# A selective-scan and attention kernel: the state input product on GpSimd, exp(delta A) in PSUM, y summed by plain matmuls

## The chip, the core and the metric

The kernel runs on one core of a Trainium2 chip, in fp32 throughout. The metric is device time in microseconds (us) of one launch. The engines are named as the profile names them: PE is TensorE (PEld its weight loads), DVE is VectorE, ACT is ScalarE, POOL is GpSimd, and SP is SyncE, whose queue issues most of the DMA.

## The reference, cut to what matters

```python
# per image of 8, over the 1024 pixels as a sequence; run forward and, flipped, backward
u, z     = split(rmsnorm(x) @ in_proj)                 # 384 channels each
u        = silu(causal_conv1d(u, 4 taps) + bias)
dt, B, C = split(u @ x_proj)                           # 24, 16 and 16 columns
delta    = softplus(dt @ dt_proj + b)
for each of 16 states n, along the sequence t:
    h[n] = exp(delta * A[n]) * h[n] + (delta * u) * B[n]
    y   += h[n] * C[n]
y        = (y + u * D) * silu(z);  global = y @ out_proj
local    = sigmoid(depthwise_conv3x3(x_norm) + b) * x_norm
x        = x + res_scale * (scale_mod * (fwd + bwd) + local)
# then, on tokens: layernorm, causal attention with RoPE, residual; layernorm, FFN 384-1536-384, residual
```

There are 8 images of 384 channels by 32 x 32 pixels. The change lies in the conv1d, in the loop over states, and in what leads from y to the output projection.

## The kernel before, in words

Channels lie on the partitions: 384 channels are NC = 3 blocks (`cc`) of P = 128. The 1024 positions of an image are two halves of HB = 512. `STEPS` names the four scan steps of an image: forward over half 0 and half 1, then backward over half 1 and half 0. The numbers 0 to 3 (`si`) are these steps. Each step goes through NS = 16 states, so that the whole kernel has 32 steps and 512 states.

One state in `scan` is this. ACT writes `da` = exp(delta * A[n]), three 128x512 activations (L346) into an SBUF tile with two buffers. DVE multiplies `du` = delta * u by B[n] over all three blocks at once (L348, 128x1536). Here B[n] is spread over the partitions by PE transposes into the PSUM bank `bb` (L335). DVE then runs three 512-long scans in place (L356). In steps 0 and 2 a small copy keeps the last column for the next step (L359). DVE multiplies by C[n] from PSUM bank `cb` (L360). Last, PE adds the product into the PSUM tile `y` by twelve 128x128 transposes that accumulate (L365), so that `y` comes out with positions on the partitions.

`prepare` makes the inputs of the next step. It computes the conv1d on PE as four matmuls with diagonal matrices for each block (L266), then silu on ACT (L270), the projection to dt, B and C, and delta through Abs, Relu, Exp and Ln (L295 to L302) and an add on DVE (L305). `gate` computes silu(z) (L247, L251). `project` transposes the gated y back (L378, L381) and applies the output projection (L386, L388). `local` is the 3x3 convolution on DVE (L228). The attention and the FFN of the image before are the generator `tail`.

The scan calls `pump` after each state. It advances the generators beside it: one step each of `prepare` and, in steps 1 and 2, of `local`, and three of `tail`. The framework orders each engine's instructions ahead of time from priorities (order in the program) and from when buffers come free[...]. Tiles with one tag share that tag's buffers. The PSUM pools take eight 512-column tiles (banks): three for `y`, one each for `bb` and `cb`, and three for everything else (`bank()`, tag `w`).

The y tile of one step is followed at its end by these lines, which also take the PE between steps:

```python
if si >= 2:
    szf = sz.rearrange("p i c -> p (i c)")
    nc.vector.scalar_tensor_tensor(szf, yv, gs, szf, ALU.mult, ALU.mult)
    ...
    project(b, h, sz, t1)
```

Of the kernel before, what the change touches and what calls it, by code (L numbers as in the profile page):

```python
# [24 lines left out]

P = 128
HB = 512
STEPS = [(0, 0), (0, 1), (1, 1), (1, 0)]


@with_exitstack
def conv_attn_kernel(
# [36 lines left out]
    l1 = ctx.enter_context(tc.tile_pool(name="l1", bufs=1))  # L69
    ps_y = ctx.enter_context(tc.tile_pool(name="ps_y", bufs=1, space=bass.MemoryType.PSUM))  # L70
    ps_b = ctx.enter_context(tc.tile_pool(name="ps_b", bufs=1, space=bass.MemoryType.PSUM))
    ps_w = ctx.enter_context(tc.tile_pool(name="ps_w", bufs=3, space=bass.MemoryType.PSUM))

    count = [0]

    def name(s):
        count[0] += 1
        return f"{s}_{count[0]}"
# [52 lines left out]

    nc.scalar.activation(nega, nega, AF.Exp)
    nc.vector.tensor_scalar_mul(nega, nega, -1.0)


    cdiag = const.tile([P, NC, 4, P], F32, name="cdiag")
    for cc in range(NC):
        for k in range(4):
            nc.gpsimd.tensor_scalar(cdiag[:, cc, k], ident, cw[:, cc, k : k + 1], None, ALU.mult)


    ddiag = const.tile([P, NC, P], F32, name="ddiag")
# [96 lines left out]

    def gate(b, h):  # L240

        sz = l0.tile([P, NT, C], F32, tag="sz", name=name("sz"))
        for i in range(NT):
            pz = bank()
            at = h * HB + i * P
            for cc in range(NC):
                nc.tensor.matmul(  # L247
                    pz[:, :C], xn_t[b][:, cc, at : at + P], win[:, cc, C:],
                    start=cc == 0, stop=cc == NC - 1,
                )  # L250
            nc.scalar.activation(sz[:, i], pz[:, :C], AF.Silu)  # L251
        return sz


    def prepare(b, step, res):

        d, h = step
        t0 = h * HB
        u = u_t[b]
        uc = l0.tile([P, NC, HB], F32, tag="uc", name=name("uc"))  # L260
        for cc in range(NC):
            pc = bank()
            for k in (3, 2, 1, 0):
                s = k - 3 if d == 0 else 3 - k
                a, e = max(t0, -s), min(t0 + HB, L - s)
                nc.tensor.matmul(  # L266
                    pc[:, a - t0 : e - t0], cdiag[:, cc, k], u[:, cc, a + s : e + s],
                    start=k == 3, stop=k == 0,
                )
            nc.scalar.activation(uc[:, cc], pc, AF.Silu, bias=v_cb[:, cc : cc + 1])  # L270
            yield
        px = bank()
        for cc in range(NC):
            nc.tensor.matmul(px[:NX], xp[:, cc], uc[:, cc], start=cc == 0, stop=cc == NC - 1)
        xd = l0.tile([NX, HB], F32, tag="xd", name=name("xd"))
        nc.scalar.copy(xd, px[:NX])
        yield

        pt = bank()
        for i in range(NT):  # L280
            nc.tensor.transpose(
                pt[:, i * NX : (i + 1) * NX], xd[:, i * P : (i + 1) * P], ident[:NX, :NX]
            )
        bc = l0.tile([P, NT, 2 * NS], F32, tag="bc", name=name("bc"), bufs=2)
        nc.scalar.copy(bc, pt[:, : NT * NX].rearrange("p (i e) -> p i e", i=NT)[:, :, R:])
        yield

        dl = l0.tile([P, NC, HB], F32, tag="dl", name=name("dl"), bufs=2)
        sps = []
        for cc in range(NC):  # L290
            pd = bank()
            nc.tensor.matmul(pd, dtw[:, cc * P : (cc + 1) * P], xd[:R], start=True, stop=True)
            sp = l0.tile([P, HB], F32, tag="tmp", name=name("sp"), bufs=4)
            bias = v_dtb[:, cc : cc + 1]
            nc.scalar.activation(sp, pd, AF.Abs, bias=bias)  # L295
            nc.scalar.activation(dl[:, cc], pd, AF.Relu, bias=bias)  # L296
            sps.append(sp)
            yield
        for sp in sps:
            nc.scalar.activation(sp, sp, AF.Exp, scale=-1.0)  # L300
        for sp in sps:
            nc.scalar.activation(sp, sp, AF.Ln, bias=ones[:, 0:1])  # L302
        yield
        for cc, sp in enumerate(sps):
            nc.vector.tensor_add(dl[:, cc], dl[:, cc], sp)  # L305
        res.append((uc, bc, dl))

    carry = const.tile([P, NS, NC], F32, name="carry")

    def block(y, i, cc):  # L310

        return y[:, i * C + cc * P : i * C + (cc + 1) * P]

    def opens(i, cc):

        return (i * C + cc * P) % HB == 0

    def scan(step, prep, y, first, last, save, restore, pump):

        d, h = step  # L320
        uc, bc, dl = prep
        du = l0.tile([P, NC, HB], F32, tag="du", name=name("du"))
        nc.vector.tensor_mul(du, dl, uc)
        for i in range(NT):
            for cc in range(NC):
                nc.tensor.matmul(  # L326
                    block(y, i, cc), uc[:, cc, i * P : (i + 1) * P], ddiag[:, cc],
                    start=first and opens(i, cc), stop=False, skip_group_check=True,
                )

        def spread(what, at):

            pb = ps_b.tile([P, HB], F32, tag=what, name=name(what))
            for i in range(NT):
                nc.tensor.transpose(  # L335
                    pb[:, i * P : (i + 1) * P],
                    bc[:, i, at : at + 1].to_broadcast([P, P]),
                    ident,
                )
            return pb.unsqueeze(1).to_broadcast([P, NC, HB])  # L340

        bb, cb = spread("bb", 0), spread("cb", NS)
        for n in range(NS):
            da = l0.tile([P, NC, HB], F32, tag="da", name=name("da"), bufs=2)
            for cc in range(NC):
                nc.scalar.activation(da[:, cc], dl[:, cc], AF.Exp, scale=nega[:, cc, n : n + 1])  # L346
            hs = l0.tile([P, NC, HB], F32, tag="hs", name=name("hs"), bufs=3)
            nc.vector.tensor_mul(hs, du, bb)  # L348
            if n + 1 < NS:
                bb = spread("bb", n + 1)  # L350
            for cc in range(NC):
                o, a = hs[:, cc], da[:, cc]
                if d:
                    o, a = o[:, ::-1], a[:, ::-1]
                init = carry[:, n, cc : cc + 1] if restore else 0.0
                nc.vector.tensor_tensor_scan(o, a, o, init, ALU.mult, ALU.add)  # L356
            if save:
                at = 0 if d else HB - 1
                nc.vector.tensor_copy(carry[:, n], hs[:, :, at])  # L359
            nc.vector.tensor_mul(hs, hs, cb)  # L360
            if n + 1 < NS:
                cb = spread("cb", NS + n + 1)
            for cc in range(NC):
                for i in range(NT):
                    nc.tensor.matmul(  # L365
                        block(y, i, cc), hs[:, cc, i * P : (i + 1) * P], ident,
                        start=False, stop=last and n == NS - 1,
                        is_transpose=True, skip_group_check=True,
                    )
            pump()  # L370

    def project(b, h, yzT, t1):

        yz = l0.tile([P, NC, HB], F32, tag="hs", name=name("yz"), bufs=3)
        for cc in range(NC):
            pt = bank()
            for i in range(NT):
                nc.tensor.transpose(  # L378
                    pt[:, i * P : (i + 1) * P], yzT[:, i, cc * P : (cc + 1) * P], ident
                )  # L380
            nc.scalar.copy(yz[:, cc], pt)  # L381
        for i in range(NT):
            cols = slice(i * P, (i + 1) * P)
            po = bank()
# [204 lines left out]
    for b in range(NB):  # L589
# [4 lines left out]
        for si, step in enumerate(STEPS):  # L594
            d, h = step
            prep = preps.pop()
            if si == 1:
                run(rest)
                yv = y1 = ps_y.tile([P, NC * HB], F32, tag="y", name=name("y"))
            elif si == 2:  # L600
                yv = y1
            else:
                yv = ps_y.tile([P, NC * HB], F32, tag="y", name=name("y"))
            if si >= 2:
                sz = gate(b, h)
            if si == 3:
                for k in range(0, NC * HB, HB):
                    nc.tensor.matmul(
                        yv[:, k : k + HB], ident, y0[:, k : k + HB],
                        start=True, stop=False, skip_group_check=True,  # L610
                    )
            nxt = (b, STEPS[si + 1]) if si < 3 else (b + 1, STEPS[0])
            side = []
            if si == 0:
# [15 lines left out]
                if g is not local_b or si == 2:  # L630
                    run(g)
            if si == 0:
                y0 = l0.tile([P, NC * HB], F32, tag="y0", name=name("y0"))
                nc.scalar.copy(y0, yv)
            if si >= 2:
                szf = sz.rearrange("p i c -> p (i c)")
                nc.vector.scalar_tensor_tensor(szf, yv, gs, szf, ALU.mult, ALU.mult)
                if t1 is None:
                    run(tail)
                    t1 = l1.tile([P, L // P, C], F32, tag="t1", name=name("t1"))  # L640
# [78 lines left out]
```

## Time and profile before

| | |
|---|---|
| median of 3 runs | 5035.7 us (5034.59 to 5038.16) |
| the profiled execution's own time | 5038.16 us |
| its span, first to last instruction | 5036.1 us |
| DVE, PE, ACT, POOL busy in the span | 4349.1, 3936.4, 2812.2, 46.3 us |
| mean granted TensorE clock | 0.849 |
| one image in the steady state (L356 of step 0 to the next image's) | 1802.2 to 2408.7 us: 606.5 us |

"Busy" is time in which the engine ran an instruction. A group of the profile is all instructions of one source line, engine and shape, with total busy time, the mean of one in ns, and the idle time of the engine just before them with the work that ended it. On DVE, instructions run back to back overlap by some 0.1 us, so that the sum of durations is a little over the time they take. A plain fp32 matmul leaves two records in the trace, a transpose one.

### The profile page before, as it was taken

The page shows a single profiled execution, that of the slowest core. Times are in us where ns is not written, and L with a number is a line of the kernel's source. Part 1 is how long each engine was busy: PE and PEld are TensorE (multiplying, and loading weights), DVE is VectorE, ACT ScalarE, POOL GpSimd, SP SyncE. Part 2 cuts the span into 40 slices and gives each one's busy share as a digit, 9 for nine tenths or more (in the row PEclk, how much of TensorE's full clock was granted, in tenths as well). Part 3 has the DMA queues.
Part 4 walks back from the last instruction along what each step waited for, and adds up shares of the span by engine and source line. Part 5 has one row for each costly group of instructions (what it writes and reads, how often), then busy time and mean ns, then how long its engine had stood idle before and what let it go on. Part 6 is the DMA issues. An engine that isn't in the chain of part 4 may idle for free.

```text
span 5036.1 us, 44726 instructions
## 1 busy us (share of the span) xinstructions
PE 3936.4 (78%) x17360; PEld 2525.6 (50%) x17360; DVE 4349.1 (86%) x4404; ACT 2812.2 (56%) x3988; POOL 46.3 (1%) x87
## 2 busy tenths in 40 slices
PE   6757788777887778867888778887788777887777
PEld 3545554455545555455554555545554455545542
DVE  6998999889998899898898899988999889998841
ACT  4543567635685446844567446673567635685222
POOL 0000000000000000000000000000000000000000
PEclk8867898888997889878998789986898878997678
DMA  1000000000000000000000000000000000000000
GB/s 42 1 0 7 7 1 7 7 7 7 1 7 7 7 7 1 13 1 7 7 1 13 7 1 7 1 13 7 7 1 7 7 7 7 1 7 7 0 1 13
DMA packets 19289, 31.69 MB, mean 6 GB/s; under 512 B 5356, under 2 KB 6276, under 8 KB 19076
## 3 DMA queue, kind: packets, MB, share of 16 engines
q1 hardware_dynamic: 17152, 28.64, 1.6%
q8 instruction: 136, 2.23, 0.2%
q14 instruction: 77, 0.63, 0.0%
q10 hardware_dynamic: 1924, 0.19, 0.0%
HBM read 16.24 MB, written 12.58 MB: 6 GB/s over the span
## 4 chain that ended last, share of the span: by engine, by line
DVE 59%; PE 20%; ACT 12%; issue 8%; DMA 0%; ACTq 0%; DVEq 0%; POOL 0%; POOLq 0%
DVE hs L356 28%; DVE hs L360 12%; DVE hs L348 11%; ACT da L346 3%; PE w L386 3%; PE w L247 2%; DVE sg L228 2%; ACT L346 2%; PE y L365 2%; PE w L544 2%; PE y L326 1%; ACT gl L543 1%; ACT L543 1%; PE w L505 1%; PE w L555 1%
## 5 line engine op out<-in xcount | busy, mean ns | idle before, releaser
L346 ACT ACTIVATE da<-dl,nega 128x512 f32<-128x512 f32 x1536 | 1020.4, 714 | 1241.0 <-DVE hs L356 1143.6
L365 PE MATMUL y<-ident,hs 128*128 128x128 f32 x6144 | 1018.6, 328 | 110.3 <-DVE hs L360 110.3
L348 DVE TENSOR_TENSOR hs<-du,bb 128x1536 f32<-128x1536 f32 x512 | 891.5, 1741 | 212.9 <-PE bb L335 212.1
L365 PEld LDWEIGHTS y<-ident,hs 128*128 128x128 f32 x6144 | 921.2, 174 | 162.9 <-DVE hs L360 123.5
L356 DVE TENSOR_TENSOR_SCAN hs<-da,carry,hs 128x512 f32<-128x512 f32 x768 | 937.2, 1269 | 26.8 <-ACT da L346 21.1
L360 DVE TENSOR_TENSOR hs<-hs,cb 128x1536 f32<-128x1536 f32 x512 | 894.3, 1747 | 49.9 <-PE cb L335 39.8
L356 DVE TENSOR_TENSOR_SCAN hs<-da,hs 128x512 f32<-128x512 f32 x768 | 894.6, 1209 | 6.8
L335 PE MATMUL cb<-ident,bc 128*128 128x128 f32 x2048 | 404.8, 329 | 465.0 <-DVE hs L360 460.1
L335 PEld LDWEIGHTS cb<-ident,bc 128*128 128x128 f32 x2048 | 266.6, 161 | 666.3 <-DVE hs L360 628.3
L335 PE MATMUL bb<-ident,bc 128*128 128x128 f32 x2048 | 373.3, 309 | 217.9 <-DVE hs L348 203.4
L335 PEld LDWEIGHTS bb<-ident,bc 128*128 128x128 f32 x2048 | 263.1, 154 | 372.5 <-DVE hs L348 309.7
L346 ACT ACT_TABLE_LOAD x287 | 368.2, 1283 | 135.8 <-DVE hs L356 131.4
L266 PE MATMUL w<-u,cdiag 128*128 128x512 f32 (+3 forms) x768 | 360.2, 603 | 3.0 <-ACT dl L296 3.0
L228 DVE SCALAR_TENSOR_TENSOR sg<-xn,dww,sg 128x496 f32<-128x496 f32 (+3 forms) x384 | 275.2, 720 | 1.5
L544 PE MATMUL w<-gl,cp1s 128*32 128x512 f32 x384 | 217.3, 685 | 47.6 <-ACT gl L543 47.6
L505 PE MATMUL w<-v,pT 128*128 128x384 f32 x576 | 231.9, 554 | 28.2 <-ACT pT L501 26.4
L266 PEld LDWEIGHTS w<-u,cdiag 128*128 128x128 f32 x768 | 140.7, 195 | 142.3 <-issue 132.0
L203 PE MATMUL w<-xn,win 128*128 128x512 f32 x288 | 155.1, 677 | 37.4 <-DVE xn L196 37.4
L538 PE MATMUL w<-xrT,fc1s 32*128 32x512 f32 x384 | 156.0, 689 | 34.8 <-ACT xrT L533 34.5
L505 PEld LDWEIGHTS w<-v,pT 128*128 128x128 f32 x576 | 117.6, 214 | 114.8 <-ACT pT L501 42.2
L543 ACT ACT_TABLE_LOAD x106 | 136.0, 1283 | 34.7 <-PE w L538 32.7
L386 PE MATMUL w<-wout,yz 128*128 128x384 f32 x384 | 138.9, 499 | 0.0
(126 smaller groups left out, 4154.7 us busy)
## 6 DMA issues: line engine op xcount, KB each, us to landing
x<-in_x_dram SPq DMA_DIRECT2D x16, 768.0 KB, 4.4
out_dram<-os SPq DMA_DIRECT2D x48, 256.0 KB, 2.0
win<-in_in_wT_dram SPq DMA_DIRECT2D x1, 1152.0 KB, 8.4
wout<-in_out_wT_dram SPq DMA_DIRECT2D x1, 576.0 KB, 6.5
wvs<-in_wv_dram SPq DMA_DIRECT2D x1, 576.0 KB, 5.7
cs<-in_rope_dram SPq DMA_DIRECT2D x1, 512.0 KB, 7.1
fc1s<-in_fc_dram SPq DMA_DIRECT2D x1, 192.0 KB, 5.9
cp1s<-in_cp1T_dram SPq DMA_DIRECT2D x1, 192.0 KB, 6.2
```

The lines of the kernel that those rows point to most:

```text
L228: nc.vector.scalar_tensor_tensor(o, img[:, r0 + dy : r1 + dy, c0 + dx : c1 + dx], dww[:, cc, k : k + 1], o, ALU.mult, ALU.add,)
L266: nc.tensor.matmul(pc[:, a - t0 : e - t0], cdiag[:, cc, k], u[:, cc, a + s : e + s], start=k == 3, stop=k == 0,)
L335: nc.tensor.transpose(pb[:, i * P : (i + 1) * P], bc[:, i, at : at + 1].to_broadcast([P, P]), ident,)
L346: nc.scalar.activation(da[:, cc], dl[:, cc], AF.Exp, scale=nega[:, cc, n : n + 1])
L348: nc.vector.tensor_mul(hs, du, bb)
L356: nc.vector.tensor_tensor_scan(o, a, o, init, ALU.mult, ALU.add)
L360: nc.vector.tensor_mul(hs, hs, cb)
L365: nc.tensor.matmul(block(y, i, cc), hs[:, cc, i * P : (i + 1) * P], ident, start=False, stop=last and n == NS - 1, is_transpose=True, skip ...
L386: nc.tensor.matmul(po[:, :C], yz[:, cc, cols], wout[:, cc], start=cc == 0, stop=False)
L505: nc.tensor.matmul(pa[:, :C], pT[:, j * P : (j + 1) * P], v_all[:, j], start=j == 0, stop=j == ti,)
L543: nc.scalar.activation(gl, ph, AF.Gelu)
L544: nc.tensor.matmul(po[:NJ], cp1s[:, f], gl, start=f == 0, stop=f == NF - 1)
```

## The change

- The product du * B[n] moves from DVE to POOL. B[n] is no longer spread by PE. `prepare` writes the 16 rows of B to a DRAM tile `bd`, and `scan` loads two states at a time from there, spread to all partitions, into the SBUF tile `bb` (two buffers of 128 x 2 x 512).
- ACT writes each 128x512 block of exp(delta * A[n]) to one of two PSUM banks (`da`, two buffers of one block), from which the scan reads. `hs` has four buffers in place of three.
- y is summed by three 128x512 matmuls with the identity, with channels on the partitions. `gate` makes silu(z) in that layout too, and `project` needs no transposes.
- The conv1d is one `tensor_scalar` and three `scalar_tensor_tensor` of DVE for each block, in place of four matmuls; silu reads SBUF.
- du is computed at the end of `prepare` (two buffers), no longer at the start of `scan`.
- The banks for everything else (tag `w`) are two in place of three.

```diff
--- before.py
+++ after.py
@@ -25,6 +25,7 @@
 
 P = 128
 HB = 512
+NB2 = 2
 STEPS = [(0, 0), (0, 1), (1, 1), (1, 0)]
 
 
@@ -69,7 +70,8 @@
     l1 = ctx.enter_context(tc.tile_pool(name="l1", bufs=1))
     ps_y = ctx.enter_context(tc.tile_pool(name="ps_y", bufs=1, space=bass.MemoryType.PSUM))
     ps_b = ctx.enter_context(tc.tile_pool(name="ps_b", bufs=1, space=bass.MemoryType.PSUM))
-    ps_w = ctx.enter_context(tc.tile_pool(name="ps_w", bufs=3, space=bass.MemoryType.PSUM))
+    dram = ctx.enter_context(tc.tile_pool(name="dram", bufs=1, space=bass.MemoryType.DRAM))
+    ps_w = ctx.enter_context(tc.tile_pool(name="ps_w", bufs=2, space=bass.MemoryType.PSUM))
 
     count = [0]
 
@@ -133,12 +135,6 @@
     nc.vector.tensor_scalar_mul(nega, nega, -1.0)
 
 
-    cdiag = const.tile([P, NC, 4, P], F32, name="cdiag")
-    for cc in range(NC):
-        for k in range(4):
-            nc.gpsimd.tensor_scalar(cdiag[:, cc, k], ident, cw[:, cc, k : k + 1], None, ALU.mult)
-
-
     ddiag = const.tile([P, NC, P], F32, name="ddiag")
     for cc in range(NC):
         nc.gpsimd.tensor_scalar(ddiag[:, cc], ident, v_d[:, cc : cc + 1], None, ALU.mult)
@@ -239,16 +235,16 @@
 
     def gate(b, h):
 
-        sz = l0.tile([P, NT, C], F32, tag="sz", name=name("sz"))
-        for i in range(NT):
+        sz = l0.tile([P, NC, HB], F32, tag="sz", name=name("sz"))
+        for m in range(NC):
             pz = bank()
-            at = h * HB + i * P
             for cc in range(NC):
                 nc.tensor.matmul(
-                    pz[:, :C], xn_t[b][:, cc, at : at + P], win[:, cc, C:],
+                    pz, win[:, cc, C + m * P : C + (m + 1) * P],
+                    xn_t[b][:, cc, h * HB : (h + 1) * HB],
                     start=cc == 0, stop=cc == NC - 1,
                 )
-            nc.scalar.activation(sz[:, i], pz[:, :C], AF.Silu)
+            nc.scalar.activation(sz[:, m], pz, AF.Silu)
         return sz
 
 
@@ -259,15 +255,18 @@
         u = u_t[b]
         uc = l0.tile([P, NC, HB], F32, tag="uc", name=name("uc"))
         for cc in range(NC):
-            pc = bank()
-            for k in (3, 2, 1, 0):
+            nc.vector.tensor_scalar(
+                uc[:, cc], u[:, cc, t0 : t0 + HB], cw[:, cc, 3:4], v_cb[:, cc : cc + 1],
+                ALU.mult, ALU.add,
+            )
+            for k in (2, 1, 0):
                 s = k - 3 if d == 0 else 3 - k
                 a, e = max(t0, -s), min(t0 + HB, L - s)
-                nc.tensor.matmul(
-                    pc[:, a - t0 : e - t0], cdiag[:, cc, k], u[:, cc, a + s : e + s],
-                    start=k == 3, stop=k == 0,
-                )
-            nc.scalar.activation(uc[:, cc], pc, AF.Silu, bias=v_cb[:, cc : cc + 1])
+                o = uc[:, cc, a - t0 : e - t0]
+                nc.vector.scalar_tensor_tensor(
+                    o, u[:, cc, a + s : e + s], cw[:, cc, k : k + 1], o, ALU.mult, ALU.add
+                )
+            nc.scalar.activation(uc[:, cc], uc[:, cc], AF.Silu)
             yield
         px = bank()
         for cc in range(NC):
@@ -275,14 +274,17 @@
         xd = l0.tile([NX, HB], F32, tag="xd", name=name("xd"))
         nc.scalar.copy(xd, px[:NX])
         yield
+
+        bd = dram.tile([NS, HB], F32, tag="bd", name=name("bd"), bufs=2)
+        nc.sync.dma_start(bd, xd[R : R + NS])
 
         pt = bank()
         for i in range(NT):
             nc.tensor.transpose(
                 pt[:, i * NX : (i + 1) * NX], xd[:, i * P : (i + 1) * P], ident[:NX, :NX]
             )
-        bc = l0.tile([P, NT, 2 * NS], F32, tag="bc", name=name("bc"), bufs=2)
-        nc.scalar.copy(bc, pt[:, : NT * NX].rearrange("p (i e) -> p i e", i=NT)[:, :, R:])
+        bc = l0.tile([P, NT, NS], F32, tag="bc", name=name("bc"), bufs=2)
+        nc.scalar.copy(bc, pt[:, : NT * NX].rearrange("p (i e) -> p i e", i=NT)[:, :, R + NS :])
         yield
 
         dl = l0.tile([P, NC, HB], F32, tag="dl", name=name("dl"), bufs=2)
@@ -303,53 +305,46 @@
         yield
         for cc, sp in enumerate(sps):
             nc.vector.tensor_add(dl[:, cc], dl[:, cc], sp)
-        res.append((uc, bc, dl))
+        du = l0.tile([P, NC, HB], F32, tag="du", name=name("du"), bufs=2)
+        nc.vector.tensor_mul(du, dl, uc)
+        res.append((uc, bc, bd, dl, du))
 
     carry = const.tile([P, NS, NC], F32, name="carry")
 
-    def block(y, i, cc):
-
-        return y[:, i * C + cc * P : i * C + (cc + 1) * P]
-
-    def opens(i, cc):
-
-        return (i * C + cc * P) % HB == 0
-
     def scan(step, prep, y, first, last, save, restore, pump):
 
         d, h = step
-        uc, bc, dl = prep
-        du = l0.tile([P, NC, HB], F32, tag="du", name=name("du"))
-        nc.vector.tensor_mul(du, dl, uc)
-        for i in range(NT):
-            for cc in range(NC):
-                nc.tensor.matmul(
-                    block(y, i, cc), uc[:, cc, i * P : (i + 1) * P], ddiag[:, cc],
-                    start=first and opens(i, cc), stop=False, skip_group_check=True,
-                )
-
-        def spread(what, at):
-
-            pb = ps_b.tile([P, HB], F32, tag=what, name=name(what))
+        uc, bc, bd, dl, du = prep
+        for cc in range(NC):
+            nc.tensor.matmul(y[:, cc], ddiag[:, cc], uc[:, cc], start=first, stop=False)
+
+        def spread(n):
+
+            pb = ps_b.tile([P, HB], F32, tag="cb", name=name("cb"))
             for i in range(NT):
                 nc.tensor.transpose(
                     pb[:, i * P : (i + 1) * P],
-                    bc[:, i, at : at + 1].to_broadcast([P, P]),
+                    bc[:, i, n : n + 1].to_broadcast([P, P]),
                     ident,
                 )
             return pb.unsqueeze(1).to_broadcast([P, NC, HB])
 
-        bb, cb = spread("bb", 0), spread("cb", NS)
+        cb = spread(0)
         for n in range(NS):
-            da = l0.tile([P, NC, HB], F32, tag="da", name=name("da"), bufs=2)
-            for cc in range(NC):
-                nc.scalar.activation(da[:, cc], dl[:, cc], AF.Exp, scale=nega[:, cc, n : n + 1])
-            hs = l0.tile([P, NC, HB], F32, tag="hs", name=name("hs"), bufs=3)
-            nc.vector.tensor_mul(hs, du, bb)
-            if n + 1 < NS:
-                bb = spread("bb", n + 1)
-            for cc in range(NC):
-                o, a = hs[:, cc], da[:, cc]
+            if n % NB2 == 0:
+                bbt = l0.tile([P, NB2, HB], F32, tag="bb", name=name("bb"), bufs=2)
+                nc.sync.dma_start(
+                    bbt, bd[n : n + NB2].rearrange("(o k) t -> o k t", o=1).to_broadcast([P, NB2, HB])
+                )
+            das = []
+            for cc in range(NC):
+                da = ps_b.tile([P, HB], F32, tag="da", name=name("da"), bufs=2)
+                nc.scalar.activation(da, dl[:, cc], AF.Exp, scale=nega[:, cc, n : n + 1])
+                das.append(da)
+            hs = l0.tile([P, NC, HB], F32, tag="hs", name=name("hs"), bufs=4)
+            nc.gpsimd.tensor_mul(hs, du, bbt[:, n % NB2].unsqueeze(1).to_broadcast([P, NC, HB]))
+            for cc in range(NC):
+                o, a = hs[:, cc], das[cc]
                 if d:
                     o, a = o[:, ::-1], a[:, ::-1]
                 init = carry[:, n, cc : cc + 1] if restore else 0.0
@@ -359,26 +354,15 @@
                 nc.vector.tensor_copy(carry[:, n], hs[:, :, at])
             nc.vector.tensor_mul(hs, hs, cb)
             if n + 1 < NS:
-                cb = spread("cb", NS + n + 1)
-            for cc in range(NC):
-                for i in range(NT):
-                    nc.tensor.matmul(
-                        block(y, i, cc), hs[:, cc, i * P : (i + 1) * P], ident,
-                        start=False, stop=last and n == NS - 1,
-                        is_transpose=True, skip_group_check=True,
-                    )
+                cb = spread(n + 1)
+            for cc in range(NC):
+                nc.tensor.matmul(
+                    y[:, cc], ident, hs[:, cc], start=False, stop=last and n == NS - 1
+                )
             pump()
 
-    def project(b, h, yzT, t1):
-
-        yz = l0.tile([P, NC, HB], F32, tag="hs", name=name("yz"), bufs=3)
-        for cc in range(NC):
-            pt = bank()
-            for i in range(NT):
-                nc.tensor.transpose(
-                    pt[:, i * P : (i + 1) * P], yzT[:, i, cc * P : (cc + 1) * P], ident
-                )
-            nc.scalar.copy(yz[:, cc], pt)
+    def project(b, h, yz, t1):
+
         for i in range(NT):
             cols = slice(i * P, (i + 1) * P)
             po = bank()
@@ -596,19 +580,16 @@
             prep = preps.pop()
             if si == 1:
                 run(rest)
-                yv = y1 = ps_y.tile([P, NC * HB], F32, tag="y", name=name("y"))
+                yv = y1 = ps_y.tile([P, NC, HB], F32, tag="y", name=name("y"))
             elif si == 2:
                 yv = y1
             else:
-                yv = ps_y.tile([P, NC * HB], F32, tag="y", name=name("y"))
+                yv = ps_y.tile([P, NC, HB], F32, tag="y", name=name("y"))
             if si >= 2:
                 sz = gate(b, h)
             if si == 3:
-                for k in range(0, NC * HB, HB):
-                    nc.tensor.matmul(
-                        yv[:, k : k + HB], ident, y0[:, k : k + HB],
-                        start=True, stop=False, skip_group_check=True,
-                    )
+                for cc in range(NC):
+                    nc.tensor.matmul(yv[:, cc], ident, y0[:, cc], start=True, stop=False)
             nxt = (b, STEPS[si + 1]) if si < 3 else (b + 1, STEPS[0])
             side = []
             if si == 0:
@@ -630,11 +611,10 @@
                 if g is not local_b or si == 2:
                     run(g)
             if si == 0:
-                y0 = l0.tile([P, NC * HB], F32, tag="y0", name=name("y0"))
+                y0 = l0.tile([P, NC, HB], F32, tag="y0", name=name("y0"))
                 nc.scalar.copy(y0, yv)
             if si >= 2:
-                szf = sz.rearrange("p i c -> p (i c)")
-                nc.vector.scalar_tensor_tensor(szf, yv, gs, szf, ALU.mult, ALU.mult)
+                nc.vector.scalar_tensor_tensor(sz, yv, gs, sz, ALU.mult, ALU.mult)
                 if t1 is None:
                     run(tail)
                     t1 = l1.tile([P, L // P, C], F32, tag="t1", name=name("t1"))
```

## The prediction

> **What bounds the kernel now.** I read the page first: the busy shares and the costliest groups.
>
> ```profile
> PE 3936.4 (78%) x17360; PEld 2525.6 (50%) x17360; DVE 4349.1 (86%) x4404; ACT 2812.2 (56%) x3988; POOL 46.3 (1%) x87
> ...
> L346 ACT ACTIVATE da<-dl,nega 128x512 f32<-128x512 f32 x1536 | 1020.4, 714 | 1241.0 <-DVE hs L356 1143.6
> L365 PE MATMUL y<-ident,hs 128*128 128x128 f32 x6144 | 1018.6, 328 | 110.3 <-DVE hs L360 110.3
> ...
> L348 DVE TENSOR_TENSOR hs<-du,bb 128x1536 f32<-128x1536 f32 x512 | 891.5, 1741 | 212.9 <-PE bb L335 212.1
> ...
> L356 DVE TENSOR_TENSOR_SCAN hs<-da,carry,hs 128x512 f32<-128x512 f32 x768 | 937.2, 1269 | 26.8 <-ACT da L346 21.1
> L360 DVE TENSOR_TENSOR hs<-hs,cb 128x1536 f32<-128x1536 f32 x512 | 894.3, 1747 | 49.9 <-PE cb L335 39.8
> L356 DVE TENSOR_TENSOR_SCAN hs<-da,hs 128x512 f32<-128x512 f32 x768 | 894.6, 1209 | 6.8
> ...
> L346 ACT ACT_TABLE_LOAD x287 | 368.2, 1283 | 135.8 <-DVE hs L356 131.4
> L266 PE MATMUL w<-u,cdiag 128*128 128x512 f32 (+3 forms) x768 | 360.2, 603 | 3.0 <-ACT dl L296 3.0
> ```
>
> DVE is the bound: the scan and two products are 3618 of its 4349 us. ACT waits 1144 us for scans to free `da` (L346), while the scans wait 28 us for ACT (L356): today's two-state lookahead of exps hides ACT almost wholly. Next the chain that ended last, in a stretch with little beside the scan:
>
> ```profile
> 1014.61 1.73 DVE hs L360
> 1016.34 2.25 DVE hs L356 x2
> 1018.59 1.65 DVE hs L348
> ...
> 1021.48 1.73 DVE hs L360
> ```
>
> L360 recurs after 6.87 us, all DVE; L348 is 1.65 of it (1.74 less the overlap). Last, the stages of one image, steps 0 to 3 (columns: stretch, length, busy us and instructions of PE, PEld, DVE, ACT, POOL, then granted clock, DMA share, GB/s):
>
> ```profile
> 1802.20:1954.40 152.20, 133.44 (x632) 86.15 (x632) 141.13 (x176) 96.47 (x150) 1.45 (x2) 0.97 0.02 6
> 1954.40:2126.00 171.60, 140.35 (x587) 74.89 (x587) 160.76 (x177) 130.69 (x171) 3.25 (x6) 0.89 0.01 5
> 2126.00:2263.40 137.40, 99.17 (x451) 73.40 (x450) 120.42 (x110) 63.93 (x88) 0.00 (x0) 0.75 0.02 6
> 2263.40:2408.70 145.30, 110.29 (x505) 76.38 (x504) 120.97 (x89) 66.23 (x97) 0.00 (x0) 0.85 0.02 6
> ```
>
> DVE leads in each, but in step 1, which holds the FFN, ACT has 131 of 172 us and PE 140. Taking work off DVE helps steps 2 and 3 most.
>
> [...] (the L525 copy as a whole, then one of them on POOL and on DVE):
>
> ```profile
> L525 POOL COPY xr<-xr x64: 293/488/1227, 728.6 to 4995.6; 128x128 f32<-128x128 f32 x64
> ```
>
> ```profile
> 2540.74 1.16 POOL L525 COPY xr<-xr 128x128 f32<-128x128 f32 x1 [472.65 <-DVE xr L524]
> ```
>
> ```profile
> 2540.60 0.55 DVE L522 TENSOR_TENSOR xt<-xt,row_sb 128x384 f32<-128x384 f32 x1
> 2541.07 0.68 DVE L305 TENSOR_TENSOR dl<-dl,sp 128x512 f32<-128x512 f32 x1
> ```
>
> The copy can take 0.29 us; here it ends at 2541.90, 0.15 us after the second two-input DVE operation. Two such operations in a row kept it out throughout, so a run of them counts once. DVE as the loser isn't shown, since POOL does nothing long. In the new loop neither the scan (`da` in PSUM) nor L360 (`cb` in PSUM) has two SBUF inputs: the loop itself is free of the lock, the work beside it is not. [...] the carry copy (L359) may then wait too. [...] a load from 2040.42 is followed by its gelu at 2041.72.
>
> **The change part by part**, against the profiled 5038.2 us.
>
> 1. L348 leaves DVE: 512 x 1.65 = **-845**.
> 2. The conv moves to DVE: 32 steps x 3 blocks x (0.54 as L219, 3 x 0.73 as L228) = 262, less 0.09 of overlap for each of 384 instructions: **+228**. The 360 us it frees on PE are off the path.
> 3. du moves: 32 x 1.74 us on DVE as before: 0. Scan and L360 with a PSUM input: L360 takes 1747 ns and L323, with both in SBUF, 1740, so 0 to +10; I take 0. Exps into PSUM: no row shows it; ACT has slack, so -0.1 to +0.1 us each is hidden except as in step 6.
> 4. PE in a state: y was 1018.6/512 = 1.99 us and becomes 3 matmuls of two records, 6 x 360.2/768 = 2.8; `bb` goes (373/512 = 0.73). About 3.6 us with `cb`, in a DVE period of 5.2: hidden, 0. PE still makes `cb` behind project and gate at step ends. There 212 us of L348 waits for `bb` (up to 20.6 at once) go, but L360 of the first state is late next, behind the same PE queue, with about 3 to 4 us of scans done meanwhile. Project loses 12 transposes and three copies. Of 212 I take **-100** (0 to -212).
> 5. POOL: [...] Four `hs` buffers let it run three states ahead, so its length is hidden under 5.2 or more. The lock is not. In the DVE timeline of the image above I count 63 separate runs of two-input work (L196, L228, L235, L237, L305, L323, L522) and 23 carry copies apart from them. The 12 conv groups add about 12, making 98. [...] **+470**. [...] Queued behind the waiting instruction are DVE's scans, and behind them y.
> 6. Exps: the lookahead shrinks from six blocks to two. ACT leaves the exp table and returns 287 times (row L346 ACT_TABLE_LOAD). The shortest such absence, two loads and one operation, with the next exp, is 1.28 + 0.65 + 1.28 + 0.71 = 3.9 us. It starts some 0.8 us into a scan. Two full banks give DVE 2.25 us of scans, 3.9 with L360 between: 1.4 or 3.05 from that moment. DVE misses 2.5 or 0.9, some 1.4 on average: 402. Side work on DVE (731 us today and 228 more) falls into about half: **+200** (0 to 2.5 x 287 = 717).
> 7. Two banks `w`: in the FFN `po` holds one, so `ph` has one and gelus can't be paired. Table loads at L543 go from 106 towards 192: 86 x 1.4 = 120, of which **+100** with the slower attention and FFN after the last scan (0 to 200). PE then waits with y and `cb` behind `po`.
> 8. Loads of B: 256 of 512 KB spread out. An x load of 768 KB lands in 4.4 us; one is due per two states, over 10 us, and two buffers hold four states. bd is written a step ahead. SP's queue also carries 48 stores and 16 x loads, whose waits could hold a load; the two buffers cover 10 us. 0 (to +100).
>
> Sum: 5038 - 845 + 228 - 100 + 470 + 200 + 100 = 5091; I add 20 for states in which a lock wait also delays what ACT waits for: **5110**. The profiled run was 2.5 us above the median, which changes nothing at this precision.
>
> **The rivals.**
> (a) *The relief shows* (faster). Steps 1, 2 and 4 give 4321; if half of the lock waits fall where DVE would be idle anyway, and lock and exp stalls hide each other, 235 + 100 + 70 are added: **4730**. For it: ACT and PE idle much in steps 2 and 3. Against: steps 0 and 1, where runs of two-input work and table loads crowd. It decides below 717 us of new waits in all: with 300 for steps 6 and 7, below about 0.53 us per run.
> (b) *POOL's product is longer*, 5 us for its three-dimensional broadcast operand: busy 0.52 of the time, 1.3 us per run, 1020 for the lock: 4321 + 1020 + 300 = **5640**. For it: the short POOL tensor_scalar at L139 takes 0.6 us for 128 elements. [...]
> (c) *The loads come late*: 256 x 4.4 = 1126 exposed, **5900**. Against: POOL's lookahead.
> That the product isn't moved at all can't be.
>
> **How the numbers follow.** About 0.2% is what a measurement of this kernel can tell from no change. The forecast case has 0.47 (own range 4980 to 5400, of which 0.04 within 0.2% and 0.03 below), (a) 0.33, (b) 0.16, (c) 0.04. Faster 0.36, same 0.04, slower 0.60. The range must reach into (a) and up to (b): 4710 to 5610.
>
> **What would show it.** Step 1: DVE without L348[...]. Step 5: two-input DVE work (L228, L305 of before) and carry copies longer by a product's rest, or long idle before them. Step 6: scans waiting for `da` by some hundred us instead of 28, more exp table loads. Step 7: gelus one by one. Step 4: L360 waiting for `cb` at step ends. DVE in a quiet stretch at 5.2 us per state would show the relief itself; a POOL product over 4.5 us, or no lengthened DVE work, would prove step 5 wrong.

## The result and the profile after

The changed kernel takes **5267.2 us** (5263.7 to 5271.2) against 5035.7: a ratio of 1.0459, 95% interval [1.0441, 1.0477]. It is slower, as forecast, but by 231 us where the forecast had 74. The profiled execution has a span of 5261.9 us.

From the page of the kernel after: the engine totals and the groups that answer to those shown of before.

```profile
PE 4073.2 (77%) x10608; PEld 1791.6 (34%) x10608; DVE 4293.2 (82%) x4276; ACT 2871.0 (55%) x3968; POOL 1817.8 (35%) x587
...
L345 POOL TENSOR_TENSOR hs<-du,bb 128x1536 f32<-128x1536 f32 x512 | 1788.6, 3502 | 2864.4 <-PE y L359 2547.4
...
L351 DVE TENSOR_TENSOR_SCAN hs<-da,carry,hs 128x512 f32<-128x512 f32 x768 | 950.6, 1268 | 209.4 <-ACT da L342 165.1
L355 DVE TENSOR_TENSOR hs<-hs,cb 128x1536 f32<-128x1536 f32 x512 | 889.9, 1738 | 203.0 <-PE cb L325 195.9
L351 DVE TENSOR_TENSOR_SCAN hs<-da,hs 128x512 f32<-128x512 f32 x768 | 902.6, 1206 | 114.0 <-POOL hs L345 77.2
...
L527 ACT ACT_TABLE_LOAD x155 | 198.9, 1283 | 104.0 <-PE w L522 102.4
...
L307 DVE TENSOR_TENSOR dl<-dl,sp 128x512 f32<-128x512 f32 x96 | 108.8, 1141 | 66.0 <-ACT sp L304 66.0
```

DVE lost a product of 891 us and is busy only 56 us less. Its scan and its product with C keep their lengths (1268, 1206 and 1738 ns, against 1269, 1209 and 1747 before), so that no cost of the PSUM operands shows. Other DVE instructions became longer: L307, the add that was L305 at 687 ns, now takes 1141. POOL sits idle for 2864 us before its products, 2547 of them until PE has added a `y` and an `hs` buffer comes free. The waits of DVE:

```profile
DVE hs L351 <- ACT da L342: 201.6, 128, 3.7
DVE hs L355 <- PE cb L325: 195.9, 60, 15.4
DVE hs L351 <- POOL hs L345: 121.4, 37, 4.3
```

The wait for `bb` (212 us) has gone; these three, 519 us together, stand against 21, 40 and none before (the 28 us in the prediction for the scans waiting for ACT should read 21). The four steps of one image, in the columns of the table shown of before:

```profile
1854.50:2023.60 169.10, 141.65 (x425) 72.38 (x424) 136.49 (x169) 93.23 (x146) 53.33 (x19) 0.92 0.09 30
2023.60:2228.90 205.30, 162.35 (x383) 61.95 (x382) 174.90 (x181) 130.62 (x166) 67.06 (x24) 0.80 0.08 27
2228.90:2350.40 121.50, 93.84 (x243) 39.89 (x243) 111.14 (x100) 76.22 (x99) 51.96 (x15) 0.85 0.11 37
2350.40:2485.90 135.50, 101.91 (x280) 47.73 (x280) 113.49 (x87) 64.85 (x91) 54.52 (x16) 0.89 0.11 37
```

Steps 2 and 3, with little beside the scan, gained 16 and 10 us. Steps 0 and 1, with attention and FFN, lost 17 and 34: 25 us an image in the steady state. Another 62 us lie after the last scan, where no state is left: from its start to the end it is 221.8 us before and 283.8 after.

### The profile page after: what moved, and what is told of

It reads as the page before. It is cut to its first block, busy times and chain, and to the rows that moved or that the text cites. A ratio compares the mean times of both kernels' runs of the same rounds, so it can differ in the third digit from the quotient of the medians.

```text
span 5261.9 us, 32572 instructions
## 1 busy us (share of the span) xinstructions
PE 4073.2 (77%) x10608; PEld 1791.6 (34%) x10608; DVE 4293.2 (82%) x4276; ACT 2871.0 (55%) x3968; POOL 1817.8 (35%) x587
## 4 chain that ended last, share of the span: by engine, by line
DVE 47%; issue 20%; PE 19%; ACT 10%; POOL 3%; DMA 0%; ACTq 0%; DVEq 0%; POOLq 0%
DVE hs L351 19%; DVE hs L355 9%; PE y L359 6%; DVE sg L224 5%; DVE uc L266 4%; POOL hs L345 3%; PE w L528 2%; PE w L522 2%; DVE carry L354 2%; ACT da L342 2%; DVE x L233 2%; PE cb L325 1%; ACT L342 1%; PE w L489 1%; DVE uc L258 1%
## 5 line engine op out<-in xcount | busy, mean ns | idle before, releaser
L345 POOL TENSOR_TENSOR hs<-du,bb 128x1536 f32<-128x1536 f32 x512 | 1788.6, 3502 | 2864.4 <-PE y L359 2547.4
L359 PE MATMUL y<-hs,ident 128*128 128x512 f32 x3072 | 1736.8, 700 | 30.4 <-DVE hs L355 30.4
L351 DVE TENSOR_TENSOR_SCAN hs<-da,carry,hs 128x512 f32<-128x512 f32 x768 | 950.6, 1268 | 209.4 <-ACT da L342 165.1
L355 DVE TENSOR_TENSOR hs<-hs,cb 128x1536 f32<-128x1536 f32 x512 | 889.9, 1738 | 203.0 <-PE cb L325 195.9
L351 DVE TENSOR_TENSOR_SCAN hs<-da,hs 128x512 f32<-128x512 f32 x768 | 902.6, 1206 | 114.0 <-POOL hs L345 77.2
L359 PEld LDWEIGHTS y<-hs,ident 128*128 128x128 f32 x3072 | 649.9, 231 | 651.5 <-issue 599.6
L224 DVE SCALAR_TENSOR_TENSOR sg<-xn,dww,sg 128x496 f32<-128x496 f32 (+3 forms) x384 | 392.5, 1035 | 1.1
L266 DVE SCALAR_TENSOR_TENSOR uc<-u,cw,uc 128x512 f32<-128x512 f32 (+3 forms) x288 | 314.4, 1103 | 1.4
L522 PE MATMUL w<-xrT,fc1s 32*128 32x512 f32 x384 | 294.1, 854 | 9.5 <-ACT xrT L517 6.0
L527 ACT ACTIVATE gl<-w 128x512 f32<-128x512 f32 x192 | 114.6, 597 | 185.0 <-PE w L522 183.7
L370 PE MATMUL w<-wout,sz 128*128 128x384 f32 x384 | 151.1, 534 | 58.8 <-DVE sz L617 57.0
L442 PE MATMUL w<-wvs,xT 128*128 128x384 f32 x384 | 145.1, 523 | 35.1 <-ACT v L446 18.3
L307 DVE TENSOR_TENSOR dl<-dl,sp 128x512 f32<-128x512 f32 x96 | 108.8, 1141 | 66.0 <-ACT sp L304 66.0
```

Source lines behind the costliest of these rows:

```text
L224: nc.vector.scalar_tensor_tensor(o, img[:, r0 + dy : r1 + dy, c0 + dx : c1 + dx], dww[:, cc, k : k + 1], o, ALU.mult, ALU.add,)
L266: nc.vector.scalar_tensor_tensor(o, u[:, cc, a + s : e + s], cw[:, cc, k : k + 1], o, ALU.mult, ALU.add)
L345: nc.gpsimd.tensor_mul(hs, du, bbt[:, n % NB2].unsqueeze(1).to_broadcast([P, NC, HB]))
L359: nc.tensor.matmul(y[:, cc], ident, hs[:, cc], start=False, stop=last and n == NS - 1)
L522: nc.tensor.matmul(ph, fc1s[g * NJ : (g + 1) * NJ, f // NG], xrT[g * NJ : (g + 1) * NJ], start=True, stop=True,)
L527: nc.scalar.activation(gl, ph, AF.Gelu)
```

## The experiments

Two theories compete. **The lock**: GpSimd's product makes DVE's two-input work and copies wait. **The bank**: two PSUM tiles for all work beside the scan, in place of three, serialise that work. Each edit also makes the framework order all instructions anew, so that differences of some tens of us are not read closely.

### One bank less, in the kernel before (b_two_w)

```diff
-    ps_w = ... name="ps_w", bufs=3
+    ps_w = ... name="ps_w", bufs=2
```

> The kernel before with two banks w in place of three, nothing else. Theory (the lost bank was mis-sized in the prediction): the time after the last scan grows from 222 us towards the 284 us of the kernel after, gelu table loads at the FFN go from 106 to about 155, and the whole costs 80 to 150 us: 5115 to 5185. Rival (the bank is worth next to nothing, the longer end comes from the other layout or from the scheduling): 5036 plus or minus 15.

Measured: 5283.2 us, ratio 1.0483 [1.0465, 1.0500]. This one number costs more than the whole change, and more than the theory allowed. The FFN's table loads go from 106 to 162, and from the start of the last scan to the end it is 283.5 us, as in the kernel after. The FFN shows why. The first FFN half after the last scan, from its first gelu to its twelfth, in the stage columns: in before, then here, then in the kernel after:

```profile
4955.60:4985.60 30.00, 25.54 (x44) 4.88 (x44) 3.15 (x6) 8.57 (x17) 1.11 (x2) 0.65 0.00 0
```

```profile
5140.20:5191.40 51.20, 43.06 (x44) 7.48 (x44) 3.15 (x6) 9.08 (x16) 1.11 (x2) 0.50 0.00 0
```

```profile
5120.40:5171.60 51.20, 43.05 (x44) 7.46 (x44) 3.15 (x6) 9.12 (x16) 1.11 (x2) 0.50 0.00 0
```

`po` holds one bank for twelve rounds. With two more, PE fills a second `ph` while ACT works on the first, and gelus come in pairs. With one, matmul, gelu and matmul follow each other, 4.65 us a round, at a granted clock of 0.50 (0.65 in before), and PE is busy 0.98 us for each matmul record, 0.58 in before. The chain is longer at an equal clock as well. In before the clock is 0.50 in this stretch, and a pair takes 6.36 us, 3.18 a gelu:

```profile
4966.60 1.08 ACT L543 ACTIVATE gl<-w 128x512 f32<-128x512 f32 x2 [4.69 <-PE w L538]
...
4972.96 1.08 ACT L543 ACTIVATE gl<-w 128x512 f32<-128x512 f32 x2 [5.28 <-PE w L538]
```

Attention is not affected at the end: the first gelu starts 141.4, 141.9 and 142.2 us after the last scan in the three kernels. Beside the scans, DVE waits longer for what PE makes: for `bb` 259 us in place of 212, and for `cb` 131 in place of 40:

```profile
DVE hs L360 <- PE cb L335: 130.6, 21, 17.7
```

### Two blocks of exps, in the kernel before (b_short_exp)

```diff
-            da = l0.tile([P, NC, HB], ..., bufs=2)
             for cc in range(NC):
+                da = l0.tile([P, HB], ..., bufs=2)
```

> The kernel before with da as single 128x512 blocks in two SBUF buffers, so that ACT is two blocks ahead in place of six. Theory (step 6 of the prediction): scans wait for da by about 200 us in place of 28, 5180 to 5280. Rival (ACT has slack enough, since DVE needs 6.9 us per state here): under 60 us, 5036 to 5095.

Measured: 5069.3 us, ratio 1.0060 [1.0045, 1.0075]: 31 us. The rival holds, in this kernel:

```profile
DVE hs L358 <- ACT da L347: 84.6, 41, 4.4
```

In the kernel after the same wait is 201.6 us. That L348, with its 1.65 us in each state, covers ACT here and no longer there is not the main reason: with the product back on DVE (a_prod_dve, next but one) the wait is still 180.9 us. The banks are a part of it: 75.1 us with three banks `w`, 124.5 with two (a_dve_w3 and a_dve_w2, below).

### The conv1d on DVE, in the kernel before (b_conv_dve)

```diff
-                nc.tensor.matmul(pc[...], cdiag[:, cc, k], u[...], ...)
+                nc.vector.scalar_tensor_tensor(o, u[...], cw[...], o, ALU.mult, ALU.add)
```

> The kernel before with the conv1d on DVE as in the kernel after. Without long GpSimd products the operations should have their free lengths (scalar_tensor_tensor 0.73 us where the kernel after shows 1.10). Theory (step 2): plus 228, 5220 to 5290. Rival (part of it falls into idle time of DVE, 687 us of the span): plus 100 to 180.

Measured: 5113.1 us, ratio 1.0148 [1.0133, 1.0163]: 75 us, below the rival's range. The operations have their free lengths (535 and 741 ns), and DVE is busy 214 us more, so two thirds went into its idle time: the waits for `bb` fall from 212 to 171 us, among others.

### The product back on DVE, in the kernel after (a_prod_dve)

```diff
-            nc.gpsimd.tensor_mul(hs, du, bbt[...])
+            nc.vector.tensor_mul(hs, du, bbt[...])
```

> The kernel after with the product du B on DVE, from the same SBUF tiles; all else as after. It undoes the move to GpSimd alone. Theory (lock and lateness of the product take back most of the gain): DVE gets 845 us, loses about 550 us of lengthened instructions and 121 us of waits for POOL: 5400 to 5470. Rival (the lock is small, something else ate the gain): 5267 plus about 800, 6000 or more; or the lock is worse than what the product costs, then below 5267.

Measured: 5239.3 us, ratio to before 1.0396 [1.0380, 1.0411]. This is below the theory's range, and 28 us below the kernel after, whose interval begins at 1.0441. A new order of instructions could make that much, so the reading is: **the move to GpSimd by itself gains nothing**. Against this kernel, DVE's groups in the kernel after other than scans and products are 556 us longer in sum (L224 by 123, L266 by 105, the carry copies by 102), and the 121 us of waiting for POOL are new. The wait for exps stays:

```profile
DVE hs L351 <- ACT da L342: 180.9, 121, 3.4
```

### The product left out, GpSimd writes only (a_memset)

```diff
-            nc.gpsimd.tensor_mul(hs, du, bbt[...])
+            for _ in range(3):
+                nc.gpsimd.memset(hs, 0.01)
```

> The kernel after with the GpSimd product left out: GpSimd writes the same tile hs with three memsets, which read nothing from SBUF (the scan input is a constant, du and B are not used in it). GpSimd still writes each tile and takes a few us per state. Theory (the lock on SBUF reads lengthens DVE's two-input work by some 550 us): scalar_tensor_tensor back to 0.73 us and the tensor_tensor of L307 to 0.69; the carry copies may still be long; DVE busy falls by 350 to 550 us. The time falls by 150 to 400 us, as far as DVE and not the two banks w set it: 4870 to 5120. Rival (the lengthening is under other waits): DVE busy falls, the time stays within 60 us of 5267.

Measured: 4747.5 us, ratio 0.9435 [0.9421, 0.9449], 520 us below the kernel after and beyond the theory's range. GpSimd is busy longer than with the product (2110 against 1789 us), yet two-input work is free again (L224 711 ns and L307 686, where the kernel after has 1035 and 1141), and copies (386 ns, 163 in before) and the conv's `tensor_scalar` (731 ns, 535 when free) are not. The page, then the group of the carry copy:

```profile
PE 3922.7 (83%) x10608; PEld 1720.0 (36%) x10608; DVE 3804.4 (80%) x4276; ACT 2860.0 (60%) x3961; POOL 2139.8 (45%) x1611
...
L346 POOL MEMSET hs<- 128x1536 f32 x1536 | 2110.3, 1381 | 2183.8 <-PE y L360 2112.9
...
L224 DVE SCALAR_TENSOR_TENSOR sg<-xn,dww,sg 128x496 f32<-128x496 f32 (+3 forms) x384 | 268.4, 711 | 1.1
```

```profile
L355 DVE COPY carry<-hs 128x3 f32<-128x3 f32 x256 | 98.9, 386 | 3.1
```

So the product, which reads SBUF, lengthens DVE's two-input work, and memsets, which only write, leave it at its lengths of before (720 and 687 ns). The 520 us hold one thing more: a memset waits for neither du nor B, and is late for the scans by 13 us where the product is by 121. How much of that lateness comes from the lock is not shown. One wait can be seen in the kernel after. First DVE, then POOL:

```profile
2460.24 0.67 DVE L307 TENSOR_TENSOR dl<-dl,sp 128x512 f32<-128x512 f32 x1
...
2464.86 2.14 DVE L307 TENSOR_TENSOR dl<-dl,sp 128x512 f32<-128x512 f32 x1
```

```profile
2463.02 7.27 POOL L345 TENSOR_TENSOR hs<-du,bb 128x1536 f32<-128x1536 f32 x2 [4.62 <-PE y L359]
```

With POOL idle the add takes 0.67 us. The second one meets a product that takes 3.43 us and ends at 2466.5; the add ends 0.5 us later, at 2467.0, and only then do the scans go on.

### The carry by a reduction (a_carry_red)

```diff
-                nc.vector.tensor_copy(carry[:, n], hs[:, :, at])
+                nc.vector.reduce_max(carry[:, n], hs[:, :, at : at + 1], axis=AX.X)
```

> The kernel after with the carry copy made by a reduction over one element (reduce_max) instead of a copy. Theory (the copy [...] waits for the product, a reduction does not): its mean falls from 559 to about 165 ns, 100 us less DVE work, time 5170 to 5230. Rival (any read of hs waits, as the wait is for something else): mean stays near 560 ns, time 5267 plus or minus 15.

Measured: 5155.2 us, ratio 1.0247 [1.0232, 1.0262]: 112 us from one line, more than the theory's 37 to 97. The group in the kernel after, then here:

```profile
L354 DVE COPY carry<-hs 128x3 f32<-128x3 f32 x256 | 143.1, 559 | 2.6
```

```profile
L354 DVE TENSOR_REDUCE carry<-hs 128x3 f32<-128x3 f32 x256 | 36.6, 143 | 2.6
```

The copy's median in the kernel after is 168 ns, but its longest 3377: most are free, and some wait for nearly a whole product (3502). Engine and data are the same; only the kind of instruction differs. Why the copy waits and the reduction does not is not shown.

### B by loads, in the kernel before, with the freed bank given to w (b_load4, b_load3)

B goes through DRAM as in the change, one state per load; the product stays on DVE; `da` is five one-block buffers to make room.

```diff
-            nc.vector.tensor_mul(hs, du, bb)
-            if n + 1 < NS:
-                bb = spread("bb", n + 1)
+            nc.vector.tensor_mul(hs, du, bbt[...])
-    ps_w = ... bufs=3
+    ps_w = ... bufs=4
```

> The kernel before with B spread by loads from DRAM (one state per load, two buffers), the product still on DVE; the bank bb is given to w, which has four; da as five blocks to make room. Theory (the banks w and PE's bb work at step ends are what counts): the 212 us of waiting for bb go in part, PE loses 373 us: 4830 to 4950. Rival (DVE is the bound and nothing else matters): 5000 to 5036; or loads arrive late: above 5036.

> As b_load4 (4818) with three banks w in place of four. Theory (loads of B relieve PE's queue and make up most of its gain): 4830 to 4900. Rival (the fourth bank is the gain): 4980 to 5030.

Measured: with four banks **4818.0 us**, ratio 0.9577 [0.9563, 0.9592], faster than both kernels and just below the theory's range; with three 4874.6, ratio 0.9675 [0.9659, 0.9692], as its theory has it. Loads, with the other split of `da`, thus bring some 160 us and the fourth bank some 50 more. The engine totals with four banks:

```profile
PE 3606.7 (75%) x15312; PEld 2328.3 (48%) x15312; DVE 4313.2 (90%) x4404; ACT 2843.3 (59%) x3971; POOL 44.3 (1%) x87
```

PE has 330 us less to do, and DVE, with the same work as before, is at 90% instead of 86%: the waits for `bb` at step ends are gone, and those for `cb` are 71 us. A load of 256 KB lands in 3.3 us.

### The same with the product on GpSimd (b_load4_pool)

```diff
-            nc.vector.tensor_mul(hs, du, bbt[...])
+            nc.gpsimd.tensor_mul(hs, du, bbt[...])
```

> As b_load4 with the product on GpSimd, so that banks don't limit, but with da in SBUF: now each scan has two SBUF inputs. Theory (the lock holds for scans too: 3.5 us of product and 3.4 us of scans exclude each other in each state, with 1.65 us for the product with C free beside): at least 7 us per state as before and waits on top, 5100 to 5700, scans with a mean well over 1.3 us. Rival (scans don't take the lock): scans at 1.2 to 1.27 us and a time near 4300 to 4600.

Measured: 5336.3 us, ratio 1.0604 [1.0587, 1.0622]. With enough banks, GpSimd's product costs 518 us against DVE's. `da` is in SBUF, and the scans show it:

```profile
L366 DVE TENSOR_TENSOR_SCAN hs<-da,carry,hs 128x512 f32<-128x512 f32 x768 | 1262.3, 1683 | 137.2 <-POOL hs L360 137.2
L366 DVE TENSOR_TENSOR_SCAN hs<-da,hs 128x512 f32<-128x512 f32 x768 | 1196.5, 1601 | 76.0 <-POOL hs L360 65.7
```

They take 0.4 us more than in b_load4, without GpSimd's product (1265 and 1205 ns), and than with `da` in PSUM beside it (1268 and 1206). Writing exps to PSUM does keep the scan out of the lock, but the two banks it takes are those that the FFN needs.

### The bank in the layout of the kernel after (a_dve_w2, a_dve_w3)

Product on DVE, `da` in two one-block SBUF buffers, three `hs` buffers; then the third bank w.

```diff
-                da = ps_b.tile([P, HB], F32, tag="da", ...)
+                da = l0.tile([P, HB], F32, tag="da", ...)
-    ps_w = ... bufs=2
+    ps_w = ... bufs=3
```

> The kernel after with the product on DVE, exp(delta A) back in SBUF (two one-block buffers as in PSUM) and three hs buffers, still two banks w. Control for the next run, 5239 with the product on DVE alone: within 40 us of it, unless where the exps are written matters.

> As the control, with three banks w (the two PSUM banks of da are free). Only the banks differ. Theory (the third bank is worth in the layout of the kernel after what it is worth in that of before, 245 us): time after the last scan back from 283 to about 222 us, 180 to 250 us off the control, 4990 to 5060. Rival (the cost of the bank overlaps the other costs in this layout): only the 60 us at the end, about 5175.

Measured: 5270.6 and 5065.5 us, ratios 1.0463 [1.0448, 1.0479] and 1.0056 [1.0041, 1.0071]. The control is 31 us above a_prod_dve, from which two edits part it (`da` in SBUF, three `hs` buffers). The third bank is worth **205 us** here, 61 of them after the last scan (284.0 to 223.0 us). What it is worth beside GpSimd's product and exps in PSUM was not run; that takes nine banks, and the pools here have eight.

### The conv1d back on PE, in the kernel after (a_best1, a_red_hs3)

Both have the carry by a reduction and three `hs` buffers; a_best1 also has the conv of the kernel before.

```diff
-            hs = ... bufs=4
+            hs = ... bufs=3
-                nc.vector.scalar_tensor_tensor(o, u[...], cw[...], o, ALU.mult, ALU.add)
+                nc.tensor.matmul(pc[...], cdiag[:, cc, k], u[...], ...)
```

> The kernel after with the conv1d back on PE, the carry by a reduction, and three hs buffers to make room. Theory (the conv of DVE costs its operations plus what the lock adds to them, 390 us in the profile with the wait before them): 5155 less 200 to 350, so 4800 to 4950. Rival (two banks w bind, and the conv on PE needs them too, or three hs buffers make the product late): above 5020.

> The kernel after with the carry by a reduction (5155) and three hs buffers in place of four; conv1d on DVE. It splits a_best1 (5282). Theory (three buffers make the product late, because each waits for a later y): scans wait for POOL by about 250 us as in a_best1 instead of 123, time 5240 to 5300. Rival (the conv on PE, with its need of w banks and its place in PE's queue, is what costs): 5155 plus or minus 30, waits for POOL near 123 us.

Measured: 5282.0 us with the conv on PE, 5228.7 without, against 5155.2 with four buffers and the conv on DVE. The theory of a_best1 fell and its rival's range holds: 395 us less work on DVE and a longer time. The buffer accounts for 74 us (its waits for POOL are 164 us, not the 250 expected, and its time is just below the theory's range), the conv on PE for 53 more, which is near what a new order could make. The waits of DVE in a_best1:

```profile
DVE hs L358 <- PE cb L328: 397.0, 118, 19.1
DVE hs L354 <- ACT da L345: 274.8, 172, 4.7
DVE hs L354 <- POOL hs L348: 248.2, 152, 4.3
```

DVE waits 397 us for `cb` in place of 213 in a_red_hs3. That this comes from PE's queue and from the two banks that the conv now needs as well is argued, not shown.

## Why the prediction was off

The direction was right, and so was the lock as a cost: beside the product L307 went from 687 to 1141 ns and the carry copy from 163 to 559. The size was off by a factor of three. The two banks (step 7) were priced far too low; the errors of steps 1, 2, 4 and 6 nearly cancelled. By its steps:

1. *L348 leaves DVE, -845*: the work left, but not that much time. From a_prod_dve to a_memset DVE is busy 757 us less and the kernel is 492 us faster. Most of the rest went into longer waits, for exps (180.9 to 308.0 us) and for `cb` (98.7 to 156.1). In a_memset 76 us of lengthened copies and `tensor_scalar` remain. The step took DVE's work for time.
2. *Conv, +228*: its work was counted rightly (DVE 214 us busier in b_conv_dve), but alone it cost 75, since DVE had idle time to take it. In the kernel after the lock lengthened it to 389 us (L258 and L266).
3. *PSUM operands, 0*: right (1738 ns at L355; an exp takes 690 ns into PSUM, and 720 into SBUF in a_dve_w2).
4. *Step ends, -100*: the 212 us for `bb` went, and `cb` was late in their place, 40 to 196 us. That leaves -56. PE's matmuls for y take 3.4 us a state where 2.8 was estimated; what this new form of y costs was not run alone.
5. *Lock, +470*: 520 by a_memset, lateness included. The product's length behind the forecast was the author's estimate; no trace of before shows it. The kernel after gives numbers to work with: a product takes 3.50 us, and products fill 0.36 of the 4978 us up to the last scan. If each of the 98 runs meets one at that share and waits half of it, an estimate from these is 0.36 x 1.75 = 0.63 us a run, and 98 x 8 x 0.63 = 494: the right order. For the 23 carry copies of an image the same working gives 23 x 8 x 0.63 = 116 us, and a_carry_red gained 112. What it missed is that the product itself can be late: 121 us, which the prediction put at nothing because of four buffers. Rival (b), a product of 5 us, did not occur.
6. *Exps, +200*: scans wait 180 us more for ACT than before, near the forecast, but the working does not explain them. In before the same lookahead of two blocks costs 31 us. In a_prod_dve, with the long state, the waits are 180.9 us already, so that the shorter state adds 21. A third bank takes off 49 (a_dve_w3); the rest is open.
7. *Two banks w, +100*: **the step that failed.** Alone it costs 245 us in before, and 205 in a layout close to the kernel after. The prediction counted the additional table loads (162 and 155 were measured, where it went to 192 at most) and priced each at a stall of 1.4 us; for b_two_w's 56 that would be 78 of the 245 us. It named the slower FFN after the last scan and the PE waiting behind `po`, but set them at almost nothing. The serial chain through one bank is 62 us after the last scan, where the loads play no part (six in either kernel), and b_two_w's waits for `bb` and `cb` are 138 us longer.
8. *Loads, 0*: right; 512 KB land in 3.6 us, and no wait for them shows.

The runs form a chain from before to after. a_dve_w3 has all of the change but the product on GpSimd, the exps in PSUM, the fourth `hs` buffer and the lost bank. The next kernels lose the bank, then get exps in PSUM and the buffer, then have the product taken off DVE without reads, then the product's reads.

| kernel | us | difference | forecast for it |
|---|---|---|---|
| before | 5035.7 | | |
| a_dve_w3 | 5065.5 | +30 | +328 (steps 2, 4, 6) |
| a_dve_w2 | 5270.6 | +205 | +100 (step 7) |
| a_prod_dve | 5239.3 | -31 | 0 (step 3) |
| a_memset | 4747.5 | -492 | -845 (step 1) |
| after | 5267.2 | +520 | +470 (step 5) |

Steps 1, 2, 3, 4 and 6 together were forecast at -517 and came to -493. That is luck: DVE's relief brought 353 us less than forecast, and the edits beside it cost 298 us less. What did not cancel is the bank, 105 us over its forecast, and the lock, 50 over. The shares hold for this order of edits; another order could share the same total otherwise, and +30 and -31 are no more than a new order of instructions can make. Rival (a) needed new waits below 717 us in all; lock and bank alone make 725.

## What to carry to other kernels

Before PSUM tiles are given to a new use, find the chains beside the main loop that hold one tile while cycling through the others, and count what is left for them: here the third tile was worth 205 to 245 us, as much as the whole change cost. A product on GpSimd that reads SBUF was paid for by the two-input and copying DVE instructions beside it (520 us, lateness included); keep the main loop's operands in PSUM, worth 0.4 us a scan beside the product, only if that space is free, and try a reduction for a tiny copy (143 ns in place of 559). Work taken off the busiest engine is not time gained one to one: here 757 us of DVE's work were worth 492. Spreading a row by loads from DRAM, with the product left on DVE, relieved TensorE of 330 us and freed a bank at once (4818.0 us).

## What the runs showed of the hardware

- PE's granted clock was 0.50 while the FFN went gelu by gelu (b_two_w and after), and 0.65 and 0.83 in the two FFN halves after the last scan where gelus came in pairs (before).
- A 128x3 copy on DVE took 386 ns as a mean beside GpSimd memsets of 1381 (a_memset), 559 beside the products (after) and 163 in before, where GpSimd does next to nothing; as a reduction it took 143 beside the products (a_carry_red).
- A scan with one operand in PSUM and one in SBUF took 1206 and 1268 ns beside the GpSimd product (after). With both in SBUF it took 1601 and 1683 beside the product (b_load4_pool), 1205 and 1265 without it (b_load4).
